# Layer two's first pass: the stores of the turned adjacency blocks are issued by ScalarE in place of GpSimd

## The chip, the core and the metric

The kernel runs on one core of a Trainium2 chip. That core has five engines with an instruction list each: TensorE (PE, matmuls and transposes; its weight loads are shown apart as PEld), VectorE (DVE), ScalarE (ACT), GpSimd (POOL) and SyncE (SP, which here issues loads and the final stores). A DMA is issued by an engine's list and carried out by 16 DMA engines. Instructions of one list start in order; between lists there are semaphores. The metric is the device time of one launch in microseconds (us).

## The reference

Sixteen graphs of 1024 nodes with 128 features go through two layers. Each layer takes relu of a layer norm and adds the result of a graph network to its input. The second layer's network is the one the change touches:

```python
adj_d = _dilate(adj, mask)                       # adj * keep, keep is 0 or 1
h1 = _bn(relu(_sage(x,  adj_d, Wr1, Wx1, b1, mf)), g1, be1)
h2 = _bn(relu(_sage(h1, adj_d, Wr2, Wx2, b2, mf)), g2, be2)
h3 = _bn(relu(_sage(h2, adj_d, Wr3, Wx3, b3, mf)), g3, be3)
out = (concat([h1, h2, h3]) * mf @ Wl + bl) * mf
```

with

```python
def _sage(x, adj, Wr, Wx, b, mf):
    deg = clip(sum(adj, -1, keepdims=True), 1.0, None)
    agg = einsum('bij,bjd->bid', adj, x) / deg
    out = agg @ Wr + x @ Wx + b
    return out / max(norm(out), 1e-12) * mf[..., None]
```

`_dilate` walks through a graph's rows one by one, removes some neighbours of each and takes them out of the matching columns too. The pattern of what is kept is symmetric; the weights of the adjacency are not. All of layer two uses the same masked adjacency three times, and `_bn` normalises over all graphs, so a pass over all sixteen must end before the next can use its result.

## The kernel before

A graph's adjacency is cut into 8 x 8 blocks of 128 x 128 (64 KB each in float32). `B` is 16 graphs, `NCH` is 8 block rows, `CPH` is 4 blocks.

*First part (to about 1535 us).* Layer one runs together with the dilation. It leaves in DRAM the pattern of what is kept (`keep_d`, half precision) and the transposed blocks of the upper triangle (`adjT_d`).

*First pass of layer two (about 1540 to 2150 us).* One round per graph `b`, eight steps per round, one for each block row `q`. A row tile `aT` holds, for block row q, first the 8 - q transposed blocks from the diagonal on (loaded from `adjT_d`, L396), then the 7 - q plain blocks right of the diagonal (loaded from the input adjacency, L398). There are two sets of row tiles, for even and odd graphs. A step does this:

- `masked` (L1409): TensorE transposes the pattern's blocks (L1416), VectorE multiplies them with the pattern itself (L1418) and masks both halves of `aT` in place (L1424 and L1428).
- `turn` (L1433), one step later: TensorE transposes the 7 - q plain masked blocks, up to four to a PSUM tile (L1441); ScalarE copies each PSUM tile back over them (L1442). Then the masked row goes to DRAM for the later passes in two stores: the first 8 - q blocks as one piece of a row of `adT_d[b][q]` (L1443), and the 7 - q turned blocks, each into the column q of a row block further down (L1445), in pieces of 512 bytes. Both are issued by GpSimd. A graph has 8 stores of the first kind and 7 of the second, of 7, 6, 5, 4, 3, 2 and 1 blocks: 28 blocks or 1.84 MB.
- `follow` (L1451), two steps later: TensorE multiplies the row with the projected features (`agg`, L1199), 129 columns wide, so that the degree comes out beside the sums. When a group of rows is complete, VectorE weighs the sums (L1221 to L1225); after the last row GpSimd stores the reciprocal degrees (`rd`, L1234, 1024 pieces of 4 bytes). `norms` has ScalarE square the rows (L1113), and VectorE, ScalarE (L367) and VectorE (L369) form the reciprocal lengths, with which VectorE scales them (L1132).
- From step 3 on the previous graph's output is turned and kept (`keep`, L1138 and L1140), and with the row tiles that are still there the *next* layer's sums are formed (`onward`, L1253 and L1261). ScalarE evicts them (L1161), GpSimd stores them (L1164). These matmuls are the last readers of a row tile: when they are through, SP may load the row of the graph after next into it.

Per graph SP issues 8 loads of the pattern (L407), one of the features (`hN`, L409) and 15 of row tiles; the features are loaded in pieces of 512 bytes.

*Later passes (from 2150 us).* The second pass reads whole rows of `adT_d` (L1281), multiplies them with the second layer's output (`sumb`, L1536) and takes up the sums of the first pass as `A`. The third part forms the output.

*Order.* The first part's instructions are put in order by the kernel's own planner. From there on the framework orders each engine's list: it goes through the program with a model of when each instruction could start, so a list need not follow the program's order. GpSimd's list, for instance, takes the row store of block row q + 1 before the store of the turned blocks of row q. The framework also sets all semaphores. The records of the DMA issues show that SP's DMAs take eight completion semaphores in turn, and GpSimd's another eight; before an issue the list waits until that semaphore's previous DMA has landed. No DMA is issued by ScalarE anywhere.

Of the kernel before, what the change touches and what calls it, by code (L numbers as in the profile page):

```python
# [259 lines left out]
def tile_adj_preln_d2(  # L260
# [40 lines left out]
    nc = tc.nc  # L301
# [111 lines left out]
    with ExitStack() as actx:  # L413
# [63 lines left out]
        class Batch:  # L477
# [100 lines left out]
            def turn(self, s, ew):  # L578

                q = SEQ[s]  # L580
                row = NCH - q
                for c in range(1, row, CPH):
                    n = min(CPH, row - c)
                    pt = ps_t.tile([P, CPH, P], F32, tag="gt", name=f"gt_{self.b}_{self.l}_{q}_{c}")
                    at = row + c - 1
                    for i in range(n):
                        nc.tensor.transpose(pt[:, i, :], ew[:, at + i, :], ident)  # L587
                    nc.scalar.activation(ew[:, at : at + n, :], pt[:, :n, :], AF.Copy)  # L588
# [497 lines left out]
    with ExitStack() as bctx:  # L1086
# [314 lines left out]
        with ExitStack() as c1:  # L1401
# [31 lines left out]
            def turn(s, q, aT):  # L1433

                b, row = s.b, NCH - q
                for c in range(1, row, CPH):
                    n = min(CPH, row - c)
                    at = row + c - 1
                    pt = ps_sm.tile([P, CPH, P], F32, tag="sm", name=f"pta_{b}_{q}_{c}")
                    for i in range(n):  # L1440
                        nc.tensor.transpose(pt[:, i, :], aT[:, at + i, :], ident)  # L1441
                    nc.scalar.activation(aT[:, at : at + n, :], pt[:, :n, :], AF.Copy)  # L1442
                nc.gpsimd.dma_start(adT_d[b][q][:, q * P :], aT[:, :row, :].rearrange("p c q -> p (c q)"))  # L1443
                if row > 1:
                    nc.gpsimd.dma_start(  # L1445
                        adT_d[b][q + 1 :, :, q * P : (q + 1) * P].rearrange("n p t -> p n t"), aT[:, row:, :]
                    )

# [13 lines left out]
            for b in range(B):  # L1462
                kb, hN = then
                hT = pool2.tile([P, NCH, P], F32, tag="hT2", bufs=1, name=f"hT1_{b}")
                transposed(ps_sm, hT, hN, f"h1{b}")
                now = First(b, hT)
                final = b == B - 1
                for q in range(NCH):
                    behind.append((now, q, masked(b, q, kb)))
                    if len(behind) > 1:  # L1470
                        turn(*behind[-2])
                    if len(behind) > LAG1:
                        follow()
                    if q == 1 and b + 1 < B:
                        then = fetch(b + 1)
                    if q == 3 and b == 0:
                        batches[-1].next_layer(poolk, pool2)
                    if not b:
                        continue
                    was = ended[b - 1] if q > 1 else None  # L1480
                    if q == 3:
                        was.keep(0)
                    if q == 4:
                        was.keep(1)
                        was.onward(0, 0, 1)
                    if q == 5:
                        was.onward(0, 2, 3)
                    if q == 6 and not final:
                        was.onward(1, 0, 1, 2, 3)
                    if q == 7 and not final:  # L1490
                        was.onward(1, 4, 5, 6, 7)
            turn(*behind[-1])
            while behind:
                follow()
# [176 lines left out]
```

## Time and profile before

| | us |
|---|---|
| median of 3 runs | 2674.16 (2670.14 to 2691.16) |
| profiled execution | 2669.1 |
| its span | 2667.4 |
| TensorE busy | 2588.9 (97%) |
| VectorE busy | 1787.9 (67%) |
| ScalarE busy | 1470.4 (55%) |
| GpSimd busy | 688.5 (26%) |
| granted TensorE clock, mean | 0.993 |
| DMA on the hardware queue | 391.7 MB, 48.0% of 16 engines' span |
| DMA on the software queue | 181.8 MB, 22.4% |

Busy times of different engines overlap. An engine's idle time costs something only if another engine is waiting for it, and what ended the idle time is inferred from semaphore events. A group's line gives source line, engine, operation, output and input, shapes and count, then busy time, the mean duration of one in ns, and the idle time just before. A line of the waits gives the waiting engine and line, the releaser, total us, times and the longest. "SPq" is SP's list of DMA issues: an issue's duration is the time that the list was held by it, not the transfer's. The hardware queue carries what SP issues, the software queue what GpSimd issues.

### The profile page before, as it was taken

The page shows a single profiled execution, that of the slowest core. Times are in us where ns is not written, and L with a number is a line of the kernel's source. Part 1 is how long each engine was busy: PE and PEld are TensorE (multiplying, and loading weights), DVE is VectorE, ACT ScalarE, POOL GpSimd, SP SyncE. Part 2 cuts the span into 40 slices and gives each one's busy share as a digit, 9 for nine tenths or more (in the row PEclk, how much of TensorE's full clock was granted, in tenths as well). Part 3 has the DMA queues.
Part 4 walks back from the last instruction along what each step waited for, and adds up shares of the span by engine and source line. Part 5 has one row for each costly group of instructions (what it writes and reads, how often), then busy time and mean ns, then how long its engine had stood idle before and what let it go on. Part 6 is the DMA issues. An engine that isn't in the chain of part 4 may idle for free. (4 is left out here: it accounts for less than half of the span.)

```text
span 2667.4 us, 48644 instructions
## 1 busy us (share of the span) xinstructions
PE 2588.9 (97%) x16761; PEld 1992.4 (75%) x16761; DVE 1787.9 (67%) x4799; ACT 1470.4 (55%) x4209; POOL 688.5 (26%) x1141
## 2 busy tenths in 40 slices
PE   8999999999999999999999999999999999999978
PEld 6777777777777777777776789889889865655678
DVE  3767778777877789788784465555546545565565
ACT  6868687577666676575563333323333335555565
POOL 4122222122221222222220132333323322222460
PEclk9999999999999999999999999999999999999999
DMA  9457386285565587584642099999999979999427
GB/s 291 142 177 225 102 253 199 64 254 176 139 211 136 166 254 169 149 258 121 177 152 101 17 307 293 319 278 291 317 276 287 278 213 377 347 348 331 155 80 222
DMA packets 400705, 576.70 MB, mean 216 GB/s; under 512 B 87809, under 2 KB 277249, under 8 KB 400449
## 3 DMA queue, kind: packets, MB, share of 16 engines
q1 hardware_dynamic: 348416, 391.72, 48.0%
q0 software_dynamic: 52032, 181.78, 22.4%
q8 instruction: 135, 2.21, 0.3%
q14 instruction: 122, 0.99, 0.1%
HBM read 369.89 MB, written 188.81 MB: 209 GB/s over the span
## 5 line engine op out<-in xcount | busy, mean ns | idle before, releaser
L558 PE MATMUL pg<-nhT 128*128 128x512 f32 (+3 forms) x1152 | 445.9, 490 | 11.1 <-DVE ew L570 7.1
L598 PE MATMUL po<-ew,hS 128*128 128x512 f32 (+3 forms) x1152 | 445.2, 491 | 6.1 <-PEq L1071 3.6
L570 DVE TENSOR_TENSOR ew<-pg,adjA 128x768 f32<-128x768 f32 (+3 forms) x528 | 430.0, 824 | 1.0 <-PE pg L558 0.8
L612 PEld LDWEIGHTS po<-ew,hS 128*128 128x128 f32 x2688 | 338.7, 192 | 39.2 <-issue 38.3
L612 PE MATMUL po<-ew,hS 128*128 128x128 f32 x2688 | 366.5, 276 | 0.0
L588 ACT ACTIVATE ew<-gt 128x512 f32<-128x512 f32 (+1 forms) x480 | 209.3, 467 | 234.3 <-PE gt L587 229.0
L535 POOL TENSOR_TENSOR hS<-hN,rn 128x128 f32<-128x128 f32 x384 | 169.3, 474 | 481.3 <-DVE rn L369 360.2
L598 PEld LDWEIGHTS po<-ew,hS 128*128 128x128 f32 x1152 | 193.8, 191 | 94.9 <-issue 62.9
L567 DVE TENSOR_TENSOR ew<-pg,adjA 128x128 f32<-128x128 f32 x384 | 108.3, 282 | 226.3 <-PE pg L558 151.2
L558 PEld LDWEIGHTS pg<-nhT 128*128 128x128 f32 x1152 | 187.2, 191 | 94.9 <-issue 65.9
L1199 PE MATMUL agg<-hw,aT 128*128 128x129 f32 x2048 | 257.8, 276 | 0.0
L1199 PEld LDWEIGHTS agg<-hw,aT 128*128 128x128 f32 x2048 | 241.2, 191 | 0.0
L587 PEld LDWEIGHTS gt<-ident,ew 128*128 128x128 f32 x1344 | 165.7, 141 | 96.9 <-issue 74.0
L1536 PE MATMUL sumb<-aT,o 128*128 128x512 f32 x512 | 225.5, 593 | 1.8 <-ACT o L1130 1.8
L587 PE MATMUL gt<-ident,ew 128*128 128x128 f32 x1344 | 208.7, 274 | 1.8 <-DVE ew L570 1.4
L1442 ACT ACTIVATE aT<-pta 128x512 f32<-128x512 f32 (+3 forms) x160 | 71.2, 467 | 205.9 <-PE pta L1441 194.1
L1536 PEld LDWEIGHTS sumb<-aT,o 128*128 128x128 f32 x512 | 94.6, 190 | 109.2 <-issue 99.2
L532 ACT ACTIVATE hS<-hN 128x128 f32<-128x128 f32 x384 | 114.6, 302 | 77.6 <-DVE hN L516 62.7
L475 POOL DMA_DIRECT2D adjT<-adjA x128 | 70.6, 552 | 335.6 <-ACT adjA L474 295.8
L1418 DVE TENSOR_TENSOR both<-pkb,kb 128x1024 f16<-128x1024 f16 (+7 forms) x128 | 57.6, 450 | 147.7 <-PE pkb L1416 128.9
L1253 PE MATMUL next<-aT,o 128*128 128x512 f32 (+3 forms) x384 | 151.1, 497 | 0.0
L974 ACT ACTIVATE kp<-rank,fin 128x1024 f16<-128x1024 uint8 x128 | 146.7, 1150 | 6.7 <-DMA keep<-kp 5.1
(213 smaller groups left out, 5054.5 us busy)
## 6 DMA issues: line engine op xcount, KB each, us to landing
an<-in_adj_dram SPq DMA_DIRECT2D x128, 512.0 KB, 5.0
aT<-adT SPq DMA_DIRECT2D x128, 512.0 KB, 8.9
keep<-kp POOLq DMA_DIRECT2D x128, 256.0 KB
kb<-keep SPq DMA_DIRECT2D x128, 256.0 KB, 6.5
sum<-sum POOLq DMA_DIRECT2D x64, 256.0 KB
A<-sum SPq DMA_DIRECT2D x32, 512.0 KB, 4.1
xb<-in_x_dram SPq DMA_DIRECT2D x31, 512.0 KB, 4.6
adT<-aT POOLq DMA_DIRECT2D x32, 448.0 KB
```

The costliest lines, as they stand in the source:

```text
L532: nc.scalar.activation(hS[:, c, :], self.hN[:, c, :], AF.Square, accum_out=ss[:, c : c + 1])
L535: nc.gpsimd.tensor_tensor(hS[:, c, :], self.hN[:, c, :], self.rn[:, c : c + 1].to_broadcast([P, D]), ALU.mult)
L558: nc.tensor.matmul(pg[:, :n, :].rearrange("p c q -> p (c q)"), lhsT=self.nhT[:, q * P : (q + 1) * P], rhs=self.nhT[:, (q + c) * P : (q + c ...
L570: nc.vector.tensor_tensor(both[0][:, :, off, :], pg[:, own:n, :].unsqueeze(1).to_broadcast([P, 2, n - own, P]), both[1][:, :, off, :], ALU ...
L587: nc.tensor.transpose(pt[:, i, :], ew[:, at + i, :], ident)
L588: nc.scalar.activation(ew[:, at : at + n, :], pt[:, :n, :], AF.Copy)
L598: nc.tensor.matmul(self.po[:, c * P : (c + n) * P], lhsT=self.hS[:, q, :], rhs=ew[:, c - q : c - q + n, :].rearrange("p c q -> p (c q)"), ...
L612: nc.tensor.matmul(self.po[:, q * P : (q + 1) * P], lhsT=self.hS[:, q + n, :], rhs=ew[:, NCH - 1 - q + n, :], start=False, stop=closes and ...
L974: nc.scalar.activation(kp, rank if exact else rank.bitcast(U8).rearrange("p (c l) -> p c l", l=2)[:, :, i % 2], AF.Abs, bias=shift[:, i : ...
L1199: nc.tensor.matmul(self.place(c), lhsT=aT[:, blk, :], rhs=self.hw[:, source, :], start=source == 0 and c % self.ga == 0, stop=c == q and s ...
L1253: nc.tensor.matmul(self.bank[:, (c - h * CPH) * P :], lhsT=self.o[:, q, :], rhs=aT[:, c - q : hi - q, :].rearrange("p c q -> p (c q)"), st ...
L1536: nc.tensor.matmul(banks[h], lhsT=now.o[:, q, :], rhs=aT[:, h * HALF : (h + 1) * HALF], start=q == 0, stop=q == NCH - 1,)
```

## The change

The second store of `turn`, that of the turned blocks, is issued from ScalarE's list in place of GpSimd's. Source, destination and shape stay; the row store (L1443) stays with GpSimd. ScalarE's list has the copies from PSUM (L1442) whose output the store reads.

```diff
@@ -1442,7 +1442,7 @@
                     nc.scalar.activation(aT[:, at : at + n, :], pt[:, :n, :], AF.Copy)
                 nc.gpsimd.dma_start(adT_d[b][q][:, q * P :], aT[:, :row, :].rearrange("p c q -> p (c q)"))
                 if row > 1:
-                    nc.gpsimd.dma_start(
+                    nc.scalar.dma_start(
                         adT_d[b][q + 1 :, :, q * P : (q + 1) * P].rearrange("n p t -> p n t"), aT[:, row:, :]
                     )
```

## The prediction

> **What bounds the kernel now.** The change sits in the first pass of layer two, 1540 to 2150 us of the span, so I first read the busy time by stretches over that pass and over pieces of one batch (its work repeats every 39.4 us). Columns: stretch, length, PE busy, weight loads, VectorE, ScalarE, GpSimd, granted clock, DMA share, GB/s.
>
> ```profile
> 1540.00:2150.00 610.00, 608.81 (x4733) 541.99 (x4732) 347.15 (x969) 193.43 (x599) 190.32 (x299) 1.00 1.00 293
> ```
>
> ```profile
> 1970.00:1975.00 5.00, 5.00 (x50) 4.89 (x48) 3.92 (x13) 1.74 (x7) 2.94 (x5) 1.00 1.07 376
> 1975.00:1980.00 5.00, 5.00 (x44) 4.74 (x42) 3.76 (x11) 2.43 (x9) 1.30 (x2) 1.00 1.19 55
> 1980.00:1985.00 5.00, 5.00 (x47) 4.94 (x46) 1.34 (x3) 0.49 (x1) 0.66 (x1) 1.00 0.90 171
> ```
>
> TensorE is busy 608.8 of 610 us at full clock; its list of waits for 1600 to 2100 us is empty. ScalarE works 32% of the pass, GpSimd 31%. The DMA engines look full too, but their rate falls from 376 to 55 GB/s while TensorE works on: the dip follows the store of the reciprocal degrees (L1234, 4-byte pieces) in every batch. So TensorE is the bound, and a gain must come out of 1.2 us.
>
> The waits of the pass (total us, times, longest) say who stands behind the moved stores:
>
> ```profile
> SPq L396 <- PE next L1253: 255.9, 14, 20.5
> ```
>
> ```profile
> POOL adT L1445 <- ACT aT L1442: 100.4, 38, 7.0
> ```
>
> ```profile
> DVE aT L1428 <- DMA aT<-in_adj_dram: 15.5, 13, 4.1
> ```
>
> SP's loads wait for TensorE to free the row tiles, not for the stores. GpSimd waits for ScalarE's evictions before the moved store, and has time to. VectorE waits once a batch for a load caught in the dip (block row 5: its product ends at 1984.1, TensorE needs it at 1986.5).
>
> **Removed.** Seven issues a batch on GpSimd, of this group (busy, mean ns, idle before):
>
> ```profile
> L1445 POOL DMA_DIRECT2D adT<-aT x88 | 68.8, 782 | 160.8 <-ACT aT L1442 100.4 <-issue 31.5 <-DMA rd<-invdeg 18.5
> ```
>
> 7 x 0.78 = 5.5 us a batch, 112 issues, 86 us in all. Behind them on GpSimd stand only other stores and a memset; in the whole span those who waited for L1445 waited under 4 us together, ScalarE 1.2 of them. Worth nothing.
>
> **Added.** Seven issues a batch on ScalarE. The trace has no DMA issued there; the nearest rows are SP's issues of 512-byte pieces (hN, L409: median 0.377 us). 7 x 0.38 = 2.7 us a batch, 43 us over the pass, in an engine idle 26 of 39 us. What counts is where they fall. Call the store of row block q's turned blocks Tq. ScalarE in the tight part of a batch (start, duration, idle before):
>
> ```profile
> 1966.51 0.98 ACT L1442 ACTIVATE aT<-pta 128x512 f32<-128x512 f32 x2 [3.92 <-PE pta L1441]
> 1968.86 0.60 ACT L1442 ACTIVATE aT<-pta 128x512 f32<-128x512 f32 x1 [1.37 <-PE pta L1441]
> ...
> 1969.64 0.38 ACT L1442 ACTIVATE aT<-pta 128x256 f32<-128x256 f32 x1
> 1969.91 0.31 ACT L1113 ACTIVATE hw<-o 128x128 f32<-128x128 f32 x1
> ...
> 1970.54 0.21 ACT L367 ACTIVATE ss<-ss 128x4 f32<-128x4 f32 x1 [0.24 <-DVE ss L366]
> 1971.98 0.77 ACT L1442 ACTIVATE aT<-pta 128x512 f32<-128x512 f32 x2 [1.23 <-PE pta L1441]
> 1974.54 0.60 ACT L1140 ACTIVATE hR<-pt_r 128x512 f32<-128x512 f32 x1 [1.79 <-PE pt_r L1138]
> 1975.20 0.60 ACT L1442 ACTIVATE aT<-pta 128x512 f32<-128x512 f32 x1
> ```
>
> T0 falls at 1967.5, in a 1.37 us gap; T2 at 1972.8, in 1.79 us; T3 at 1975.8, 2.3 us before the next instruction; T4 (1982.4), T5 (1987.5) and T6 (1992.4) have 4.2, 4.6 and 1.7 us. These hide 0.38 us each. T1 does not surely: it is due at 1970.1 to 1970.5, next to the square root L367, and VectorE stands behind that root in order:
>
> ```profile
> 1970.41 0.82 DVE L1428 SCALAR_TENSOR_TENSOR aT<-aT,both 128x640 f32<-128x640 f32 x1
> 1971.15 0.17 DVE L369 RECIPROCAL rn<-ss 128x4 f32<-128x4 f32 x1
> ...
> 1973.26 0.68 DVE L1428 SCALAR_TENSOR_TENSOR aT<-aT,both 128x512 f32<-128x512 f32 x1
> ```
>
> The last of these ends at 1973.94 and TensorE turns its product at 1974.56: 0.6 us to spare, and the root has 0.4 us before L369. So a delay of L367 up to about 1 us is free and beyond that TensorE stops. An issue of 0.38 us alone costs nothing; with its wait for the eviction before it and for a completion semaphore I take 1.3 us, that is 0.3 us on the path, in the 15 batches that have the root there: **+5 us**. Bounds: 0, and the longest issue on SP in this pass, 4.26 us behind a store-sized list of 512-byte pieces:
>
> ```profile
> 1576.78 0.78 SPq L409 DMA_DIRECT2D hN<-h  x1
> 1577.61 4.26 SPq L396 DMA_DIRECT2D aT<-adjT  x1
> ```
>
> That bound gives 4.26 + 0.2 - 1.0 = 3.5 us x 15 = 53 us. I stay near the low end, since of the 15 issues behind an hN load in the pass 12 took 0.8 to 1.5 us and two less, all within 1.3 us of that load, and T1 comes 2.6 us after T0.
>
> The Trainium skill, Perfetto Trace Analysis, section "DMA Instruction — HWDGE (DVE, Sync)", speaks against the change: one descriptor generator serves both hardware-issuing sequencers, and the second waits for a lock. By that rule T1 would also wait out an SP issue, 0.32 to 0.43 us in these rows, some 6 us more in the pass; no row of this trace has two issuers to show it.
>
> **Moved past queues.** The stores leave GpSimd's queue. In the trace's packets GpSimd's 512-byte pieces travel joined, mostly as 4096 bytes; SP's go as 512 bytes, 32.5 ns each (16,536 in 1600 to 2100 us). A batch's 28 blocks of 64 KB are 3584 such packets, 3584 x 32.5 / 16 = 7.3 us of all engines, against 448 packets of 4096 bytes at 182 ns (layer one) to 279 ns (here) = 5.1 to 7.8 us: between -0.5 and +2.2 us of transfer time a batch. The cover is SP's 20 us standstill before every batch's loads; if the loads were late by all of 2.2 us instead, block row 2 (landed 1967.3, multiplied from 1969.1) would still have 1.9 us. I take 0. Without T0 ahead of it, the degree store and the dip start about a microsecond sooner; the load for row 5 then ends no later.
>
> SP's loads take eight completion semaphores in turn, and an issue waits until that semaphore's last DMA has landed (GpSimd has eight others). If ScalarE's stores join SP's eight, each side can wait for the other: T1 for a load issued eight places before it, which landed at 1969.9 in this batch (T1 due 1970.1 or later: inside my 1.3 us), and the seventh mask load of the next batch for T6, 5.2 us after its issue (GpSimd's landing), about 0.8 us late, inside the 1.9 us of row 2. I take 0 of this beyond T1, and keep 3.3 us a batch (5.2 - 1.9) as its upper end.
>
> **Ends.** TensorE waits 3.8 us at the start of the second pass, for the sums' load caught in the last dip. The degree store stays where it is, so 0; at most -4.
>
> **Sum.** Profiled execution 2669.1 us (span 2667.4): +5 = 2674. The runs shown have median 2674.2, 5 us above the profiled one, so I predict **2679 us**. One per cent, 27 us, is about what a measurement of this kernel can tell from no change.
>
> **Rivals.**
> 1. *T1 holds ScalarE* (slower). If an issue on ScalarE blocks while the queue still has T0's 56 pieces per engine to place, L367 comes late and VectorE and TensorE with it; it decides from 1 us of delay on, and costs over 1% from about 2.8 us (27 / 15 + 1.0). For it: the 4.26 us row, and 0.6 us of slack. Against: T1 meets a queue of its own with T0 alone in it. Price 53 us: 2727. Chance 0.17.
> 2. *The shared semaphores hold the loads* (slower): 3.3 x 15 = 50 us, 2724. Against: all waits but T1's and T6's meet DMAs that landed long before. Chance 0.08.
> 3. *A small gain*: the dip takes less from the loads, and the idle 1.2 us and the 3.8 us go, with up to 5 us from GpSimd's earlier row stores at the end: 2664 to 2674. TensorE's 99.8% forbids more inside the pass. Chance 0.18.
> 4. *The change doesn't do what it says*: the framework orders each engine's list anew and may put the stores far behind their evictions, or shift other work in the later passes by a few us either way; 2669 to 2689. Chance 0.10.
>
> My forecast, 2674 to 2700, has 0.44; some 0.03 is left for anything else. The range takes in rival 3 at its low end and rival 1's price at the high end: **2664 to 2727**. Faster by over 1%: 0.03. Slower by over 1%: rivals 1 and 2 nearly whole, 0.24. Within 1%: 0.73.
>
> **What the changed profile would show.** Right: the moved line as ScalarE issues of about 0.4 us, the period still 39.4 to 40 us, TensorE's share of the pass 99% or more, L1445's GpSimd group gone with nothing earlier for it, 57,344 packets of 512 bytes more on a hardware queue. Wrong by rival 1: ScalarE issues of several us at T1 or T2, VectorE waiting for ScalarE at L369, TensorE for L1428 at L1441. By rival 2: SP waiting for the moved store ahead of the mask or row loads, VectorE waiting longer for `aT` loads. A time below 2664 would mean that TensorE was held by something that its busy time conceals.

## The result, and the profile after

| | before | after |
|---|---|---|
| median (lowest to highest), us | 2673.72 (2667.29 to 2691.16, 6 runs) | 2793.36 (2788.74 to 2797.14, 6 runs) |
| ratio, 95% interval | | 1.0449 (1.042 to 1.0478) |
| profiled execution, its span, us | 2669.1, 2667.4 | 2791.9, 2790.2 |
| TensorE busy, us | 2588.9 | 2615.6 |

The changed kernel is 4.5% slower, by 120 us. My prediction was 2679 us, in a range of 2664 to 2727. It was wrong: the measured time lies 66 us above the range.

The first pass is where it happens. Busy time by stretches of the changed kernel (columns as in the prediction: stretch, length, PE, weight loads, VectorE, ScalarE, GpSimd, granted clock, DMA share, GB/s):

```profile
1540.00:2150.00 610.00, 523.23 (x3858) 465.37 (x3857) 278.27 (x782) 158.85 (x498) 82.02 (x153) 0.92 0.88 246
```

TensorE was busy 608.8 us of this stretch before; now it idles 87 us, and the granted clock is 0.92. A batch takes 48.0 us (median of the distances between degree stores, batches 2 to 14, counted from 0) in place of 39.4. Batch 1 keeps its old length (39.5), and batch 0 ends 10 us later (its degree store is issued at 1584.6 in place of 1574.6). The waits of 1540 to 2290 us (total us, times, longest) give the order of blame:

```profile
ACT hR L1140 <- DMA adT<-aT: 172.3, 13, 15.3
...
DVE stats L1141 <- ACT hR L1140: 151.3, 14, 13.4
...
PE pta L1441 <- ACT hR L1140: 74.8, 11, 8.3
...
PE pta L1441 <- DVE invdeg L1221: 15.3, 2, 8.9
...
PE pw L1182 <- ACT hT L378: 8.5, 1, 8.5
```

Read from the top: ScalarE stands still in 13 of the 16 batches for 172 us in all, and what ends it is a *DMA of the kind that was moved* (`adT<-aT`). Behind ScalarE's eviction of `hR` wait VectorE (L1141, and in its list behind that the masks and L1221) and TensorE (L1441, the turned blocks of block row 4): 13 waits, 90.1 us. The last line is another case, in batch 0: there ScalarE's store of row 6, issued at 1571.42, had waited for the landing of row 4's, issued at 1559.15 and landed at 1571.35, and TensorE stood for 8.5 us behind it. In the trace before, TensorE had none of these 98.6 us; its list for the same stretch of time has two lines, both at the start of the second pass:

```profile
PE pw L1357 <- POOL A L1328: 3.8, 1, 3.8
PE sumb L1536 <- ACT o L1130: 1.8, 1, 1.8
```

What holds ScalarE is seen in one batch. The chain of waits of the changed kernel between 1990 and 2040 us (start, duration, what):

```profile
2013.38 17.48 DMA adT<-aT
...
2030.93 0.37 ACTq L1445
...
2031.35 0.60 ACT hR L1140
...
2033.83 0.87 PE pta L1441 x3
```

and ScalarE's own timeline there (start, duration, operation, idle before):

```profile
2017.85 0.77 ACT L1442 ACTIVATE aT<-pta 128x512 f32<-128x512 f32 x2 [1.23 <-PE pta L1441]
2030.93 0.37 ACTq L1445 DMA_DIRECT2D adT<-aT  x1
2031.35 0.60 ACT L1140 ACTIVATE hR<-pt_r 128x512 f32<-128x512 f32 x1 [12.73 <-DMA adT<-aT]
```

The evictions of block row 2 are through at 2018.6, but its store (T2, in the prediction's notation) is issued at 2030.93. It is not the issue that is slow: 0.37 us. T2 waits until row 0's store (T0), issued at 2013.38, has landed at 2030.86. The records of the DMA issues say why. Each carries the number of its completion semaphore; in the order in which the eight come round:

| issued at us | list | DMA | semaphore | landed at us |
|---|---|---|---|---|
| 2008.98 | SP | row 4, first load | 117 | 2017.99 |
| 2013.38 | ScalarE | **T0** | **101** | **2030.86** |
| 2010.65 | SP | row 4, second load | 110 | 2027.52 |
| 2012.85 | SP | row 5, first load | 111 | 2027.76 |
| 2013.76 | SP | row 5, second load | 112 | 2029.46 |
| 2014.69 | SP | row 6, first load | 113 | 2029.67 |
| 2015.91 | ScalarE | T1 | 114 | 2032.59 |
| 2017.39 | SP | row 6, second load | 115 | 2029.99 |
| 2018.06 | SP | row 7, only load | 117 | 2031.32 |
| 2030.93 | ScalarE | **T2** | **101** | 2033.53 |

SP and ScalarE draw on the same eight semaphores, the framework deals them out in the order of its list (which puts T0 ahead of SP's second load of row 4, although SP issued that one sooner), and T2 is exactly the eighth DMA after T0. T0 meanwhile lies in the dip that follows the degree store, and lands 17.5 us after its issue. Busy time by 5 us of the changed kernel, same columns:

```profile
2015.00:2020.00 5.00, 5.00 (x49) 4.89 (x48) 4.57 (x13) 2.14 (x9) 1.56 (x4) 1.00 1.10 377
2020.00:2025.00 5.00, 5.00 (x50) 4.99 (x49) 0.42 (x1) 0.00 (x0) 0.00 (x0) 1.00 1.38 61
2025.00:2030.00 5.00, 2.42 (x20) 1.97 (x18) 0.00 (x0) 0.00 (x0) 0.00 (x0) 1.00 0.86 192
2030.00:2035.00 5.00, 1.17 (x6) 1.20 (x7) 2.99 (x10) 2.22 (x6) 0.54 (x1) 0.56 0.63 195
2035.00:2040.00 5.00, 5.00 (x34) 4.95 (x34) 1.67 (x4) 1.05 (x5) 0.54 (x1) 0.75 0.31 104
```

From 2020 to 2030 VectorE, ScalarE and GpSimd do next to nothing; TensorE works ahead until 2027.4 and then stops too. When it comes back, its granted clock is 0.56 and 0.75 in the means of these two rows (0.50 from 2031 to 2037, 1.00 from 2038 on). The page "TensorE: Matmul & The Clock Gate" of the Trainium skill, section "What's actually happening", says that an idle window of about 3.4 us is enough for half the clock; the trace agrees, with a pause of 6.4 us ahead of these rows. What this costs on top of the pause shows in TensorE's busy time, which rose by 26.7 us for the same 16,761 matmuls. The account of the profiled executions: 98.6 us of new waits, less 3.4 us at the start of the second pass (5.6 us of waits before, 2.2 after), make 95; with the 26.7 us of slower matmuls that is 122, of a difference in span of 122.8.

**Theory A**: ScalarE's list is held at T2 by the semaphore that T2 shares with T0, whose landing the degree store makes late. **Theory B**: the 512-byte packets on ScalarE's own queue (57,344 of the 59,136 packets that the profile's list has for it; the others are of 4 bytes) cost the time, in proportion to the bytes moved. **Theory C**: issuing on ScalarE, or the new order of its list, costs it, in proportion to the stores.

### The profile page after: what moved, and what is told of

It is laid out like the page before. It is cut to its first block, busy times and chain, and to the rows that moved or that the text cites. A ratio compares the mean times of both kernels' runs of the same rounds, so it can differ in the third digit from the quotient of the medians.

```text
span 2790.2 us, 48403 instructions
## 1 busy us (share of the span) xinstructions
PE 2615.6 (94%) x16761; PEld 2017.6 (72%) x16761; DVE 1783.4 (64%) x4799; ACT 1468.2 (53%) x4209; POOL 598.3 (21%) x1029
## 3 DMA queue, kind: packets, MB, share of 16 engines
q10 hardware_dynamic: 59136, 29.37, 5.1%
## 4 chain that ended last, share of the span: by engine, by line
PE 31%; DMA 11%; ACT 3%; DVE 2%; issue 2%; POOL 1%; ACTq 0%; SPq 0%; POOLq 0%; DVEq 0%
DMA adT<-aT 9%; PE sumb L1536 8%; PE agg L1199 5%; PE next L1253 4%; PE pw L1182 2%; PE next L1261 2%; PE pw L1350 2%; PE po L598 1%; PE pg L558 1%; PE po L612 1%; PE pta L1441 1%; PE pw L1357 1%; DMA out_dram<-y 1%; PE pt_r L1138 1%; ACT aT L1442 1%
## 5 line engine op out<-in xcount | busy, mean ns | idle before, releaser
L1199 PE MATMUL agg<-hw,aT 128*128 128x129 f32 x2048 | 277.1, 290 | 0.0
L1199 PEld LDWEIGHTS agg<-hw,aT 128*128 128x128 f32 x2048 | 261.8, 205 | 0.0
L1141 DVE BATCH_NORM_STATS2 stats<-hR 128x6 f32<-128x512 f32 x64 | 44.2, 692 | 232.3 <-ACT hR L1140 232.3
L1140 ACT ACTIVATE hR<-pt_r 128x512 f32<-128x512 f32 x64 | 38.1, 597 | 260.3 <-DMA adT<-aT 172.3
L1443 POOL DMA_DIRECT2D adT<-aT x128 | 69.4, 542 | 489.1 <-DVE aT L1424 451.0
L1442 ACT ACTIVATE aT<-pta 128x512 f32<-128x512 f32 (+3 forms) x160 | 70.8, 464 | 168.4 <-PE pta L1441 164.4
L1441 PE MATMUL pta<-ident,aT 128*128 128x128 f32 x448 | 74.2, 291 | 90.1 <-ACT hR L1140 74.8
```

The costliest lines, as they stand in the source:

```text
L1199: nc.tensor.matmul(self.place(c), lhsT=aT[:, blk, :], rhs=self.hw[:, source, :], start=source == 0 and c % self.ga == 0, stop=c == q and s ...
```

## The experiments

### Rows 0, 1 and 2 on ScalarE

```diff
-                    nc.scalar.dma_start(
+                    (nc.scalar if q < 3 else nc.gpsimd).dma_start(
                         adT_d[b][q + 1 :, :, q * P : (q + 1) * P].rearrange("n p t -> p n t"), aT[:, row:, :]
```

> Turned-block stores of block rows 0, 1 and 2 on ScalarE, those of rows 3 to 6 back on GpSimd; nothing is left out. In the built program row 2's store still stands eight places behind row 0's among the DMAs of SP and ScalarE, so it takes the same completion semaphore and ScalarE's list waits for row 0's store to land. Theory A (that wait, 12.7 us of idle ScalarE a batch, is the whole loss): all of it stays, 2780 to 2800 us, and the group of hR L1140 still shows about 170 us of idle time behind the DMA adT<-aT. Theory B (the 512-byte packets on ScalarE's queue cost the time, by bytes): 18 of 28 blocks, so 64% of the 120 us, about 2751 us. Theory C (issuing on ScalarE, by count): 3 of 7, about 2725 us.

Measured: 2787.5 us (2780.47 to 2795.1), before on the same chip 2669.98; ratio 1.0433 (1.0402 to 1.0463). Three of the seven stores bring nearly the whole loss. Its waits:

```profile
ACT hR L1140 <- DMA adT<-aT: 168.8, 13, 14.3
```

### Rows 0 and 2 on ScalarE

The same line with `q in (0, 2)`.

> As the run with rows 0, 1 and 2 on ScalarE, but row 1's store on GpSimd too. With one DMA fewer between them row 2's store stands seven places behind row 0's and takes the semaphore of the first load of block row 4, which lands early. Theory A: the loss is gone, 2668 to 2685 us, and hR L1140 waits for no DMA. Theory B: 12 of 28 blocks, about 2725 us. Theory C: 2 of 7 stores, about 2708 us.

Measured: 2678.45 us (2672.85 to 2685.01); ratio 1.0029 (1.0012 to 1.0045). Moving T1 back took 109 us off, and the wait for a store is gone from ScalarE's list; one for a load is there twice:

```profile
ACT hR L1140 <- DMA aT<-adjT: 18.2, 2, 9.5
```

That is T2 on the semaphore of row 4's first load, which was caught in the dip in two of the batches; these two took 43.6 and 44.4 us. The first batch took 44.4 us too, with a hold of 4.9 us behind a pattern load in the list of waits; the others stand at 39.4 but for one pair of 40.8 and 38.1. So the 0.3% that is left is of the same kind. Note that T0 still landed after some 20 us here, and did no harm.

### Rows 1 to 6 on ScalarE

The same line with `nc.scalar if q else nc.gpsimd`.

> Row 0's turned-block store alone back on GpSimd, rows 1 to 6 stay on ScalarE; nothing is left out. Row 2's store then takes the semaphore of the first load of block row 4, rows 3 to 6 those of loads that in the profile before land at least 2 us ahead of the stores' places. Theory A: the loss is gone or nearly, 2668 to 2695 us (the upper end if row 3's store meets a load caught in the dip). Theory B: 21 of 28 blocks, about 2763 us. Theory C: 6 of 7 stores, about 2776 us.

Measured: 2682.32 us (2673.69 to 2688.86); ratio 1.0034 (1.0019 to 1.0048). Six of seven stores and three quarters of the bytes are on ScalarE, and of 4.5% there is 0.34% left: theories B and C are out as the cause of the 120 us. What stayed is again two single holds, one for a load, in a batch of 46.1 us, and one in the first batch:

```profile
ACT hR L1140 <- DMA aT<-adjT: 11.3, 1, 11.3
ACT hw L1113 <- DMA adT<-aT: 9.8, 1, 9.8
```

### Rows 0 and 2 on ScalarE, and one load cut in two

T1's engine was the only edit between the first two runs, so T1 itself could be the culprit. Here T1 stays on GpSimd and the count is restored by another DMA, the load of block row 5's plain blocks, which SP issues in two halves:

```diff
+        if q == 5:
+            for n in range(row - 1):
+                nc.sync.dma_start(
+                    aT[:, row + n, :], adj[b][q * P : (q + 1) * P, (q + 1 + n) * P : (q + 2 + n) * P]
+                )
-        if row > 1:
+        elif row > 1:
```

> As the run with rows 0 and 2 on ScalarE, which was as fast as the kernel before to 0.3% (2678 us against 2670 us), with one edit more: the load of block row 5's second part (two 512-byte columns) is issued by SP as two DMAs in place of one. Nothing is left out. That puts row 2's store eight places behind row 0's again, so it takes row 0's semaphore; row 1's store stays on GpSimd. Theory A (the semaphore, not which stores are on ScalarE): the whole loss comes back, 2775 to 2800 us, with some 170 us of hR L1140's idle time behind adT<-aT. Rival (row 1's store on ScalarE, by its bytes or its place ahead of the norms, was what made the difference between the two earlier runs): 2675 to 2685 us.

Measured: 2826.55 us (2816.56 to 2836.28), before on that chip 2671.31; ratio 1.0591 (1.0568 to 1.0614). Cutting one load of 128 KB in two made the kernel 148 us slower than its twin. The theory's sign is right, its size was not: I had said 2775 to 2800. The waits (five lines were added above, so L1145 is the eviction of `hR`, L1446 the turning):

```profile
ACT hR L1145 <- DMA adT<-aT: 193.0, 13, 15.6
...
PE pta L1446 <- ACT hR L1145: 75.8, 9, 9.0
...
PE pta L1446 <- DVE invdeg L1226: 35.1, 4, 9.3
```

T0 landed later in this version, T2 following it 19.9 us after T0's issue (median of batches 2 to 14) against 17.7 us in the changed kernel, and a batch took 50.7 us against 48.0. In the issue records T2 has T0's semaphore in 13 of the 16 batches here, and in none of the twin's. The cut load without the moved stores was not run.

### Row 2 back on GpSimd

The same line with `nc.gpsimd if q == 2 else nc.scalar`.

> Row 2's turned-block store alone back on GpSimd, the other six on ScalarE; nothing is left out. Now row 3's store takes row 0's semaphore. Its place is some 8.5 us behind row 0's store and row 0's lands after 17.5 us, so ScalarE is held 9 us a batch in place of 12.2. Theory A, with the loss as the hold less a slack of some 4 us: 9 less 4 is 5 us in 13 batches, 65 us, with a clock loss in the same proportion as before some 80 us: 2735 to 2765 us. If every shared hold on row 0's landing cost the same whatever its length: 2790 us. If the semaphore of row 2's store alone mattered: 2670 to 2685 us.

Measured: 2720.8 us (2714.83 to 2727.04); ratio 1.0184 (1.0161 to 1.0206). The hold moves to T3, as expected, and costs less than I had worked out:

```profile
ACT hR L1140 <- DMA adT<-aT: 129.9, 12, 13.8
```

My slack of 4 us was T2's, and too small. T3 stands later in the list, with less behind it that TensorE needs soon; that this is the reason was not tested. In this run a batch with T3 issued 16.9 to 17.7 us after T0 took 40.0 to 41.2 us; with T3 at 20.4 to 21.7 a batch took 44.9 to 46.2.

### The degree store in 32-byte pieces, with the change

The reciprocal degrees are laid out in DRAM as they lie in SBUF, eight per partition, and read back through a strided view:

```diff
-                    nc.gpsimd.dma_start(rd_d[b].rearrange("o (c p) -> p (o c)", p=P), invdeg[:, b, :])
+                    nc.gpsimd.dma_start(rd_d[b].rearrange("o (p c) -> p (o c)", p=P), invdeg[:, b, :])
...
+                    self.rd = self.rd.rearrange("x (p c) -> x c p", c=NCH)
```

> The changed kernel with the reciprocal degrees laid out in DRAM as they lie in SBUF: their store writes 128 pieces of 32 bytes in place of 1024 of 4 bytes, and the second pass reads them back through a strided view. All seven turned-block stores stay on ScalarE and row 2's still shares row 0's semaphore. Theory A, with the degree store as what makes row 0's store land after 17.5 us: the dip shrinks, row 0's store lands some 7 us after its issue, row 2's store (whose place is 5.3 us behind it) waits 2 us or less, and the time is 2665 to 2695 us. If the shared semaphore holds ScalarE but the dip has another cause: 2780 to 2800 us with the same idle time before hR L1140. Theory B or C: about 2793 us, without that idle time being tied to row 0's landing.

Measured: 2677.39 us (2672.34 to 2679.94); ratio 1.0019 (1.0005 to 1.0032). All seven stores are on ScalarE, T2 is still tied to T0, and 116 us are gone. ScalarE's timeline in one batch (L1450 is the eviction of turned blocks, L1453 the store):

```profile
1826.26 0.77 ACT L1450 ACTIVATE aT<-pta 128x512 f32<-128x512 f32 x2 [1.24 <-PE pta L1449]
1831.34 0.37 ACTq L1453 DMA_DIRECT2D adT<-aT  x1
1831.76 0.60 ACT L1140 ACTIVATE hR<-pt_r 128x512 f32<-128x512 f32 x1 [4.73 <-PE agg L1204]
```

The hold is there, 4.7 us in place of 12.7 (the line names TensorE as the releaser, but it is T0's landing, at 1831.27, that stands 0.07 us ahead of T2's issue). I had expected T0 to land after 7 us and a hold of 2 us or less; T0 landed after 10.3 (median of batches 2 to 14). TensorE hardly feels it: two waits of 0.8 and 1.0 us in the two batches with the latest T2. Against the same degree store with all stores on GpSimd (next section) 12 to 14 us are left, mainly one wait of 8.4 us in batch 0, where late stores of the same batch hold ScalarE as in the changed kernel (8.5 us). So the 8.6 us a batch need both: the shared semaphore, and a landing that comes later than what ScalarE's list has to spare. Together with the runs before, that slack can be read off, batch by batch:

| run | held store | issued after T0, us (median) | batch, us (median) |
|---|---|---|---|
| changed kernel, batches 1 and 15 (not held) | T2 | 5.3 | |
| 32-byte pieces, with the change | T2 | 10.4 | 39.4 |
| the same, its two latest | T2 | 11.9, 12.1 | 40.4, 40.6 |
| changed kernel | T2 | 17.7 | 48.0 |
| rows 0 and 2, load cut in two | T2 | 19.9 | 50.7 |
| row 2 back on GpSimd | T3 | 18.3 | 41.8 |

Up to some 11 us after T0 the hold of T2 is free, 5.7 us beyond its own place. From there on a microsecond of hold is a microsecond of batch, plus 2 us for the clock (26.7 us for 14 pauses) once TensorE's pause is long: 17.7 - 11 + 2 = 8.7 us for the changed kernel, measured 8.6 over 39.4; 19.9 - 11 + 2 = 10.9 for the load cut in two, measured 11.3. This is an estimate that fits the medians. Single batches scatter: in the changed kernel one with T2 at 18.9 us took 51.6 us, one with T2 at 19.4 took 48.0.

### The degree store in 32-byte pieces, with the kernel before

> The kernel before with the degree store of 128 pieces of 32 bytes and the strided view in the second pass; all stores of the first pass on GpSimd. TensorE is busy 608.8 of 610 us in the first pass before, so there is no idle time there for a smaller dip to give back: 2662 to 2676 us, within 0.4% of before. If the dip had cost TensorE anything in the first pass, or the read-back in the second: faster by up to 10 us. If the strided view slows VectorE's or GpSimd's product on the path: slower by up to 10 us.

Measured: 2665.78 us (2661.91 to 2668.63), before 2671.31; ratio 0.9974 (0.9958 to 0.9989). It was run once more beside the next kernel:

> The short degree store with all stores of the pass on GpSimd, once more: 2661 to 2669 us, 0.1 to 0.4% under the kernel before, if the gain of the earlier run (ratio 0.9974, 0.9958 to 0.9989) is real; within 0.1% of it, if it was that chip's.

Measured: 2663.45 us (2661.55 to 2666.91), before 2668.06; ratio 0.9979 (0.9964 to 0.9995). Both intervals end below 1: a version a little better than the kernel before, by 0.2 to 0.3% (the intervals take in 0.05 to 0.42%). Of the second of these runs, the busy times of 5 us at the place of the dip, and of the pass:

```profile
1975.00:1980.00 5.00, 5.00 (x44) 4.74 (x43) 2.71 (x9) 1.69 (x7) 1.29 (x2) 1.00 0.69 267
```

```profile
1540.00:2150.00 610.00, 608.87 (x4732) 541.96 (x4733) 346.34 (x971) 192.49 (x598) 184.57 (x299) 1.00 0.82 293
```

The same stretch moved 55 GB/s before; now 267, with the DMA engines no longer full (share 0.69 against 1.19), and the DMA share of the pass falls from 1.00 to 0.82. TensorE has nothing to gain inside the pass (608.87 us against 608.81). Outside it, its wait of 3.8 us for `A` at the start of the second pass is gone, and one of 0.9 us behind VectorE is new (L1163, whose strided product takes 1.07 us in place of 0.69). The rest of the 5 us I can't place.

### The stores on SP

`nc.sync.dma_start` in the changed line.

> The seven turned-block stores issued by SP in place of ScalarE: the same packets of 512 bytes, none of them on ScalarE's list; nothing is left out. Theory A: hR L1140 waits for no DMA any more. But in the built program row 3's store now takes row 1's semaphore, so SP's list waits there for a landing some 17 us late, and the loads of block rows 6 and 7 stand behind it: whether they are late decides, from 2670 us (they are not) to 2790 us (they hold VectorE's mask some 8 us a batch). If the packets alone were the cost, about 2793 us with no wait of either list behind it.

Measured: 2769.16 us (2764.6 to 2773.26); ratio 1.0358 (1.0339 to 1.0378). ScalarE waits for no store any more. VectorE waits for loads instead, and TensorE for VectorE:

```profile
DVE aT L1424 <- DMA aT<-adjT: 75.5, 10, 13.5
DVE aT L1428 <- DMA aT<-in_adj_dram: 56.2, 14, 9.5
```

```profile
SPq L1445 <- ACT aT L1442: 193.1, 66, 7.3
...
SPq L1445 <- DMA adT<-aT: 21.4, 12, 6.1
```

The second fence is SP's queue: ahead of the stores it waits 193 us for ScalarE's evictions, and 21 us for landings of earlier stores. My expectation put the harm on T3's wait for T1, with loads behind it. That is not how it went: in a batch read from the issue records, SP issued T0 at 1906.07, T1 at 1908.60, then row 4's second load at 1909.02 and the loads up to row 7 until 1922.3 (the last ones with issues of 2.8 and 5.6 us), and only then, at 1924.16, T3. No load stood behind the semaphore. But all loads behind T1 landed between 1924 and 1929, after the dip; in the kernel before the loads of row 4 and the first of row 5 landed ahead of it (1971.5 to 1973.7). So a list that carries both stores, which wait for evictions, and loads can make the loads late by another way; this is read from one batch and was not tested by a run of its own. What the 512-byte packets add in it can't be read from this run; the runs above show that it is little.

### Rows 1 to 6 on ScalarE, with the short degree store

Both edits from above: `nc.scalar if q else nc.gpsimd`, and the 32-byte pieces. This is the price of six issues a batch with next to no hold.

> The short degree store (128 pieces of 32 bytes), row 0's turned-block store on GpSimd, rows 1 to 6 on ScalarE: no store of ScalarE's shares a semaphore with a late landing, so what is left is the price of six issues a batch on ScalarE and of their 512-byte packets, against the run with the same degree store and all seven on GpSimd (2666 us, in the same call again). Theory A: 0 to 5 us more than that run, 2663 to 2671 us, the pass at 39.4 us a batch throughout. Rival (the issues themselves, six by 0.37 us by 16 batches, lie on the path): 35 us more, 2700 us.

Measured: 2673.61 us (2669.33 to 2676.07), beside 2663.45 for the same kernel with all seven on GpSimd: 10 us more, where I had expected at most 5. It isn't the issues, and not the dip. The steady batches take 39.4 us (but for three of 39.7, 41.0 and 37.6, which make 39.4 on the mean), and T1 to T6 stand at their old places. One hold is left, in the first batch, where the next loads compete. ScalarE there:

```profile
1558.64 0.49 ACT L1450 ACTIVATE aT<-pta 128x384 f32<-128x384 f32 x1 [2.09 <-PE pta L1449]
1568.40 0.37 ACTq L1453 DMA_DIRECT2D adT<-aT  x1
1569.12 0.31 ACT L1113 ACTIVATE hw<-o 128x128 f32<-128x128 f32 x1 [9.99 <-DMA adT<-aT]
```

T4, due at 1559.1, waits for T2 of the same batch, which landed 14.3 us after its issue, at 1568.33, on the same semaphore; TensorE waits 7.4 us for it once. I had written that no store of ScalarE's would share a semaphore with a late landing; in this one batch one did.

## Why the prediction was wrong

**What bounds the kernel: right.** TensorE was the bound, there was nothing to gain in the pass, and what the change costs is TensorE's idle time and its clock.

**The step that failed** is in the paragraph on the shared semaphores and again in rival 2: "all waits but T1's and T6's meet DMAs that landed long before", "I take 0 of this beyond T1". I had seen that the stores would join SP's eight and that each side could then wait for the other. But I counted the eight places by times of issue ("a load issued eight places before it"). By the issue times of the trace before, T0's place (1967.5) stands behind the first load of row 6, and T2 then falls on the second load of row 4, which landed at 1972.07, ahead of T2's place at 1972.8; the prediction does not write this working out. In the framework's order T0 comes ahead of the second load of row 4, and T2 falls on T0 itself. The table of semaphores shows it, and the run with one load cut in two shows that a single place decides 148 us. The numbers to price the wait were in the trace before: T0 landed there 15.7 us after its issue (issued 1968.09, landed 1983.83), and T2's place was 5 us behind it. I took 0 for a hold that would have been some 10 us, and never set it beside what ScalarE's list had to spare; the changed kernel measured 8.6 us a batch.

**The dip.** I read it as a delay of SP's loads alone, and concluded that "the load for row 5 then ends no later". It delayed the moved stores as well. In the kernel before the same tie stood on GpSimd: T4 had T0's semaphore in all 16 batches, and late landings put it 15.6 us after T0 (median), against 14.6 with the short degree store. GpSimd had time for that; ScalarE, with evictions behind T2 that others wait for, had not.

**Rival 2** named the mechanism and put it on the wrong list: SP's loads held by T6, 3.3 us a batch as an upper end, 50 us. Measured: ScalarE's list held by T0, 8.6 us a batch. As its signature I gave SP waiting for the moved store ahead of the mask loads. That is there (25.1 us in all) and harmless: with rows 1 to 6 on ScalarE it is 26.4 us, in batches of 39.4. **Rival 1** expected ScalarE's issues to be several us long at T1 or T2. They are not, as this view of the store's line in the changed kernel shows (duration of an issue in ns, least, median, longest):

```profile
L1445 ACTq DMA_DIRECT2D adT<-aT x112: 338/366/632, 1546.9 to 2273.6; - x112
```

So the 0.38 us that I took from SP's issues was right, and the 4.26 us bound never came near. T1's +0.3 us a batch, the one term of my sum, was 0: with no hold a steady batch takes 39.4 us, six issues included. The rule of descriptor generation from the Trainium skill (Perfetto Trace Analysis, section "DMA Instruction — HWDGE (DVE, Sync)"), which would have had T1 wait out an SP issue, does no visible harm either: the longest issue is 0.27 us over the median. (The section itself speaks of VectorE's and SyncE's lists; that I put ScalarE's under it was my reading.)

**The packets**: I took 0 for 512-byte pieces on a hardware queue. Six of seven stores there cost 0.34%, two holds included, so 0 stands. **GpSimd's relief**: 86 us of issues gone and nothing gained, as said. **Ends**: I took 0, at most -4; TensorE's waits at the start of the second pass fell by 3.4 us, so the low bound was nearer.

**The range.** Its upper end, 2727, was rival 1's price. No case in it let a list wait out a whole landing, and the clock's fall after TensorE's pause, a fifth of the loss, stood in no case at all.

## What to carry to other kernels

A DMA that moves to another engine can bring a wait with it that is in no line of the code: here, for the DMA eight places earlier on the semaphores that it now shares. Count those places in the order of the built program, not by issue times, and price the wait by the *landing* of that earlier DMA and by what stands behind the waiting instruction. An engine that evicts PSUM is a bad place for stores that can land late. The late landing itself, here made by a store of 1024 pieces of 4 bytes, can be the cheaper thing to mend: laying that store out in 128 pieces took 116 us off with all seven stores still on ScalarE.

## What the runs showed of the hardware

- A store of 1024 pieces of 4 bytes slows every queue, not its own alone: 55 to 61 GB/s for 5 us and T0 landing after 17.5 us. In 128 pieces of 32 bytes it landed after 6.6 us in place of 14.7 (medians of 16, both with all stores on GpSimd), the rate in that stretch was 267 GB/s, and T0, with the change, landed after 10.3 us.
- The wait for a completion semaphore stands on the issuing engine, not in the DMA queue, and it takes that engine's arithmetic with it. The Trainium skill says so, in a section on GpSimd's path (DMA: Bandwidth & Descriptors, section "🔬 Anatomy of one DMA — SWDGE (gpsimd) path": a semaphore wait happens on the issuing sequencer before the DMA is dispatched). ScalarE's 12.73 us of idle time ahead of an eviction whose input had been ready since 2020.4 show it for ScalarE, and what it is worth.
- A pause of TensorE of 6 to 9 us costs about 2 us more afterwards (26.7 us of busy time over 14 pauses, an estimate), at a granted clock of 0.56 and 0.75 in the rows from 2030 to 2040.
